# Graph layer on one core: sixteen counted groups in pairs, in slices of 20 blocks, in place of ten single ones in strips of 8

## The chip, the core and the metric

The kernel runs on one NeuronCore of a Trainium2 chip, as one launch. The time is that of the device in microseconds; of each kernel several executions are timed and their median is given. The engines are named as in the profile: PE multiplies matrices (PEld is its weight load), DVE and ACT work on vectors, POOL issues the gathers, SP issues plain transfers.

## The reference

One layer of a graph network over 12500 nodes of 256 features and 200000 edges, whose targets `dst` are sorted:

```python
h = jnp.maximum(_layernorm(x, axis=-1), 0.0)
agg = jax.ops.segment_sum(h[src], dst, num_segments=N)
z = (1.0 + eps_gin) * h + agg
t = jnp.dot(z, W1) + b1                       # 256 -> 512
t = jax.nn.relu(_batchnorm(t, g1, bt1))
conv_out = jnp.dot(t, W2) + b2                # 512 -> 256
out = x + jax.nn.relu(_batchnorm(conv_out + h, g2, bt2))
```

Each row of `agg` is a sum of the rows of h that its edges name. Rows lie anywhere in the table, so the kernel has to fetch or to count them.

## The kernel before

**Tiles and groups.** The edges are cut into 1563 tiles of 128, and these into 131 groups of 12 tiles (`GT`), one turn of the main loop each. Groups 0 to 29 (`LEAD`) gather rows of x and normalise them on ACT, while the same stage writes h into a table `h_two` of 98 blocks of 128 nodes, each feature as two f16 halves (512 columns). From group 30 on, POOL gathers from `h_two`: 12 indirect DMAs per group, 128 rows of 1 KB each (L615), into one of four buffers `gt`. `gather` is called four regular groups ahead, and its first DMA waits until PE has summed the group that held the buffer.

**A regular turn.** DVE makes one-hots `oh` of the targets two groups ahead (`edges`, L671). PE sums (`sums`, L705): 12 tiles times two halves, 24 matmuls of 128x256, weights `oh`, into a place `ps`. DVE copies the sums of the group two before to `zs` (`hold`, L764) and makes their target columns `at` (`spots`, L769); PE puts those of three before into columns (`put`, L780), DVE adds them to `zc` (`add`, L798). Each turn also forms one slice of z@W1 (`slice_of`, L808), whose statistics DVE takes (L819) and which ACT then copies out (L825) to the table `t_tab`. Puts and slices share two PSUM buffers `pz2`, so a put may have to wait until ACT has copied a slice.

**Counted groups.** Ten groups (`COUNTED`, every ninth from 41) gather nothing. For such a group PE multiplies one-hots of its edges' source blocks with one-hots of their targets, which gives a matrix of counts, and the counts with all 98 blocks of `h_two`, read in order. The work is cut into 13 strips of 8 blocks. For a strip: `mark` makes the one-hots on DVE (128x3072, L908; for the first strip of a group also L898 and L902) and has SP load 8 blocks, 1 MB, into one of three buffers (L914); `count` runs 12 matmuls of 128x256 (L927; 64 columns in the last strip) into two PSUM buffers, ACT casts both (L939); `weigh` runs 16 matmuls of 128x256 of the strip before (L958) into one PSUM total. After the last strip ACT copies the total out (L964).

**Order.** The program's order is written out by hand, one iteration per group. `RATE` of 1.6 strips per regular turn from group 31 (`BEGIN`) fixes which strips a turn has; `sums` puts the works of a turn (the puts, the slice, then count and weigh of each strip) between the tiles of its own sums on PE. A counted group's iteration has no sums. Marks of the next turn stand on DVE behind everything else of the turn. Sums are written to four places in turn, the halves of two PSUM buffers.

The lines that set the strips and the turn's works:

```python
at = {(k + 1) * n // (len(among) + 1): work for k, work in enumerate(among)}
...
spots(i - 2)
hold(i - 2)
...
upto = min(int(turns_of * RATE), len(strips))
done = sum(len(v) for v in plan.values())
plan[i] = strips[done:upto]
```

Of the kernel before, what the change touches and what calls it, by code (L numbers as in the profile page):

```python
# [18 lines left out]
P = 128  # L19
R = 4  # L20
EPS = 1e-5
GT = 12
# [8 lines left out]
COUNTED = tuple(range(41, 131, 9))  # L31
WINDOWS = 4
BLOCKS = 8
BEGIN = 31
RATE = 1.6
# [10 lines left out]
def kernel(  # L46
# [47 lines left out]
    NS = -(-NB // BLOCKS)  # L94
    c_first, c_every = COUNTED[0], COUNTED[1] - COUNTED[0]

    def counted_of(v):

        return v[:, c_first : COUNTED[-1] + 1 : c_every]

    def tiles_of(v):

        return counted_of(v[:, : NG * GT].rearrange("p (g t) -> p g t", t=GT))
# [35 lines left out]
    inner = consts.tile([P, NC, GT], F32, name="inner")  # L139
# [35 lines left out]
    vrows = consts.tile([VN, P], F32, name="vrows")  # L175
# [9 lines left out]
    with ExitStack() as es:  # L185
# [20 lines left out]
        at = 0  # L206
        for v, n in vec_list:
            nc.scalar.dma_start(vrows[at : at + n, :], v.rearrange("(k p) -> k p", p=P))
            at += n
# [49 lines left out]
        for i in range(EARLY):  # L259
# [11 lines left out]
        pw = ps_v.tile([P, NC, WINDOWS], F32, name="pw")  # L271
        nc.tensor.matmul(
            pw, lhsT=first, rhs=tiles_of(dstT).rearrange("p g (w t) -> p g w t", t=WT)[:, :, :, 0],
            start=True, stop=True,
        )
        nc.vector.tensor_tensor(
            inner.rearrange("p g (w t) -> p g w t", t=WT),
            tiles_of(dstT).rearrange("p g (w t) -> p g w t", t=WT),
            pw.unsqueeze(3).to_broadcast([P, NC, WINDOWS, WT]),
            op=OP.subtract,  # L280
        )
# [6 lines left out]
        for k, end in enumerate((P, 2 * MARGIN + 1, WD)):  # L288
# [5 lines left out]
            (inner.rearrange("p g t -> p (g t)"), 0, P, NC * GT, 2),  # L294
# [22 lines left out]

        for w in range(WINDOWS):
            side = slice(w * WD, (w + 1) * WD)
            nc.vector.scalar_tensor_tensor(  # L320
                counted_of(shift)[side], pw[side, :, w], float(-w * WD), counted_of(place)[side],
                op0=OP.add, op1=OP.subtract,
            )
# [66 lines left out]
    def fast():  # L390
# [24 lines left out]
        with ExitStack() as fs:  # L415
# [15 lines left out]
            with ExitStack() as es:  # L431
# [34 lines left out]
                near_pe = ps_i.tile([P, WIDE + NG], F32, name="col")  # L466
                col, start = near_pe[:, :WIDE], near_pe[:, WIDE:]
                nc.vector.tensor_copy(start, base)
                nc.vector.tensor_copy(col, col_i)
# [4 lines left out]
                nc.vector.tensor_scalar(shift, shift, row, None, op0=OP.add)  # L474

# [185 lines left out]
                def edges(i):  # L661
# [4 lines left out]
                    ohs[i] = sel.tile([P, GT, P], F32, name="oh", bufs=FRONT + 2)  # L666
# [995 lines left out]
```

## Time and profile before

| | before |
|---|---|
| median of 3 runs | 2405.69 us (2400.7 to 2409.59) |
| profiled execution | 2420.87 us |
| its span | 2418.9 us |
| mean granted clock of PE | 0.807 |
| first to last gather from `h_two` | 521.3 to 2194.3 us |

The profiled execution is 0.6% longer than the median. The page gives times over its span, from first to last instruction. Its part in 40 slices shows three stages: the gathers of x with the normalising (to about slice 9), the regular turns (to about slice 36), and the second product with the output. Slices are 60.5 us long; a digit is the busy share in tenths:

```profile
PE   2445565656575776677566677766767667657997
POOL 7667666675656666566656566665556656662550
PEclk9667787778687787778777887887879778779999
```

No engine stands at nine tenths in the regular turns, which makes up the most of the span. A row of groups has the line, the engine, the operation and its tiles, then after the x the count, the busy time in us, the mean ns of one, and the idle time of the engine just before with what ended it. "remote" is a release that the profile can't put down to an engine.

### The profile page before, as it was taken

To read this page: it belongs to the slowest core of one execution; us is meant where nothing else is said; L and a number is where in the kernel's file an instruction comes from. 1 tells how busy PE (TensorE), PEld (TensorE's weight loads), DVE (VectorE), ACT (ScalarE), POOL (GpSimd) and SP (SyncE) were. 2 spreads that over 40 slices of the span, in tenths; PEclk is the share of its full clock that TensorE was granted. 3 is DMA by queue.
4 is the path that set the end of the run, shared out by engine and by line. 5 is a ranking of instruction groups with operands and counts; after the bars stand their busy time and mean duration, and the time that the engine had idled before them with its cause. 6 is when DMAs were issued, how large, how long until landed. Compare 5 with 4: busy or idle time off the path is not lost.

```text
span 2418.9 us, 22189 instructions
## 1 busy us (share of the span) xinstructions
PE 1584.0 (65%) x8138; PEld 1077.9 (45%) x8138; DVE 1248.2 (52%) x1442; ACT 627.1 (26%) x1145; POOL 1451.5 (60%) x1489
## 2 busy tenths in 40 slices
PE   2445565656575776677566677766767667657997
PEld 1334454434354454445444454544434445434445
DVE  5455556545344545455354463544536455224997
ACT  4446665623111111111111111111111111102555
POOL 7667666675656666566656566665556656662550
PEclk9667787778687787778777887887879778779999
DMA  6466666554465655556456555655655556643988
GB/s 177 146 192 190 192 195 193 178 153 144 145 205 171 202 191 193 184 184 200 158 192 205 185 190 191 209 189 167 205 172 193 178 169 208 202 111 124 325 307 340
DMA packets 159092, 462.69 MB, mean 191 GB/s; under 512 B 30867, under 2 KB 58683, under 8 KB 143613
## 3 DMA queue, kind: packets, MB, share of 16 engines
q1 hardware_dynamic: 74777, 245.78, 29.3%
q0 software_dynamic: 69248, 189.16, 26.8%
q10 hardware_dynamic: 14948, 26.23, 2.9%
q8 instruction: 66, 1.08, 0.2%
q14 instruction: 53, 0.43, 0.1%
HBM read 397.00 MB, written 64.05 MB: 191 GB/s over the span
## 4 chain that ended last, share of the span: by engine, by line
PE 35%; another core or an unknown queue 27%; DVE 15%; issue 11%; ACT 10%; DMA 1%; ACTq 0%; SPq 0%; DVEq 0%
PE ps L705 8%; DVE more L908 7%; PE ph L958 6%; PE pz L808 5%; PE ph L927 4%; PE pz L780 4%; DVE oh L671 3%; ACT more L513 2%; ACT gt L513 2%; PE one L1201 2%; PE ph L808 2%; ACT gta L513 2%; PE pr L1201 1%; PE pq L1201 1%
## 5 line engine op out<-in xcount | busy, mean ns | idle before, releaser
L615 POOL DMA_INDIRECT gt<-h_two,srcT x1083 | 1025.7, 947 | 648.6 <-issue 304.5
L705 PE MATMUL ps<-gt,oh 128*128 128x256 f16 (+1 forms) x2424 | 450.6, 316 | 127.7 <-issue 114.6
L908 DVE TENSOR_TENSOR more<-col,more 128x3072 bf16<-128x3072 f32 (+1 forms) x130 | 410.3, 3166 | 231.1 <-remote 143.3
L939 ACT CAST more<-ph 128x512 f16<-128x512 f32 (+1 forms) x260 | 143.1, 562 | 1126.9 <-remote 414.5
L705 PEld LDWEIGHTS <-oh 128*128 128x128 f16 x2136 | 228.2, 108 | 234.0 <-issue 188.3
L780 PE MATMUL pz<-at,zs 128*128 128x256 f32 x476 | 169.7, 487 | 216.6 <-ACT ts L825 189.4
L764 DVE COPY zs<-ps 128x256 f32<-128x256 f32 x89 | 37.2, 418 | 498.4 <-remote 398.8
L958 PEld LDWEIGHTS <-more 128*128 128x128 f16 x1960 | 203.9, 105 | 160.3 <-issue 125.9
L958 PE MATMUL ph<-gta,more 128*128 128x256 f16 x1308 | 195.2, 297 | 73.6 <-issue 70.1
L808 PE MATMUL pz<-zc,w1s 128*128 128x512 f32 (+1 forms) x296 | 186.2, 761 | 74.9 <-DVE zc L798 52.7
L927 PE MATMUL ph<-more,more 128*128 128x256 bf16 (+1 forms) x1560 | 200.7, 277 | 33.6 <-issue 29.9
L671 DVE TENSOR_TENSOR oh<-col,dstT 128x1536 f16<-128x1536 f32 (+1 forms) x119 | 208.0, 1749 | 24.1 <-remote 17.4
L780 PEld LDWEIGHTS pz<-at,zs 128*128 128x128 f32 x476 | 107.1, 244 | 254.2 <-ACT ts L825 202.9
L615 POOL DMA_INDIRECT gt<-in_x_dram,srcT x144 | 139.9, 971 | 69.4 <-issue 39.4
L927 PEld LDWEIGHTS <-more 128*128 128x128 bf16 x1560 | 151.9, 102 | 62.9 <-issue 39.9
L808 PEld LDWEIGHTS pz<-zc,w1s 128*128 128x128 f32 x296 | 69.4, 258 | 136.0 <-issue 108.7
L958 PE MATMUL ph<-more,more 128*128 128x256 f16 x652 | 93.5, 297 | 23.1 <-issue 19.4
L798 DVE TENSOR_TENSOR zc<-pz,zc 128x512 f32<-128x512 f32 (+7 forms) x185 | 90.6, 515 | 28.6 <-remote 10.4
L808 PE MATMUL ph<-zc,w1s 128*128 128x512 f32 (+1 forms) x104 | 65.0, 753 | 56.5 <-issue 31.8
L825 ACT COPY ts<-pz 128x512 f32<-128x512 f32 x72 | 42.6, 592 | 219.1 <-DVE st L819 192.3
L615 POOL DMA_INDIRECT gta<-in_x_dram,srcT x80 | 76.5, 956 | 30.0 <-issue 16.6
L819 DVE BATCH_NORM_STATS2 st<-pz 128x6 f32<-128x512 f32 x72 | 49.8, 691 | 80.2 <-PE pz L808 31.6
(231 smaller groups left out, 1904.1 us busy)
## 6 DMA issues: line engine op xcount, KB each, us to landing
gta<-h_two SPq DMA_DIRECT2D x80, 1024.0 KB
more<-h_two SPq DMA_DIRECT2D x40, 1024.0 KB
t_tab<-ts ACTq DMA_DIRECT2D x96, 256.0 KB
gt<-h_two,srcT POOLq DMA_INDIRECT x1083
h_two<-more SPq DMA_DIRECT2D x24, 512.0 KB
h_cols<-gt SPq DMA_DIRECT2D x24, 512.0 KB
zc<-h_cols SPq DMA_DIRECT2D x24, 512.0 KB
yT<-h_cols SPq DMA_DIRECT2D x24, 512.0 KB
```

The lines of the kernel that those rows point to most:

```text
L513: nc.scalar.activation(slot(to, c), slot(v, c), AF.Relu, bias=nb[:, c : c + 1], scale=rs[:, c : c + 1])
L615: fetch = nc.gpsimd.indirect_dma_start(out=slot(ga, t - t0)[:rows], out_offset=None, in_=x if i < LEAD else h_two, in_offset=bass.Indirect ...
L671: nc.vector.tensor_tensor(oh, col[:, :P].unsqueeze(1).to_broadcast([P, n, P]), dstT[:, t0 : t0 + n].unsqueeze(2).to_broadcast([P, n, P]), ...
L705: part = nc.tensor.matmul(ps, lhsT=lhsT, rhs=side, start=(j == order[0] and side is sides[0]), stop=(j == order[-1] and side is sides[-1]),)
L780: nc.tensor.matmul(pz[:, d, :n], lhsT=zs[:, d * P : (d + 1) * P], rhs=at[:, :n], start=True, stop=True)
L798: nc.vector.tensor_add(side, pz[:, :, a - lo : b - lo], side)
L808: nc.tensor.matmul(ph[:, :n], lhsT=w1s[:, d, f * P : (f + 1) * P], rhs=zc[c][:, d, :n], start=(d == 0), stop=(d == DC - 1),)
L908: nc.vector.tensor_tensor(marks[(k * NS + s) % 3][:, :, :n], col[:, :n].unsqueeze(1).to_broadcast([P, GT, n]), keys[k % 2][:, s, :].unsque ...
L927: nc.tensor.matmul(ph[:, w * strip : w * strip + n], lhsT=low[:, j, :], rhs=marked[:, j, :n], start=(t == 0), stop=(t == WT - 1),)
L939: nc.scalar.copy(to[:, :b, 2 * v * WD : 2 * (v + 1) * WD].rearrange("p a (w d) -> p w a d", w=2), ph.rearrange("p (w a d) -> p w a d", w=2 ...
L958: nc.tensor.matmul(total, lhsT=counts[m % 2][:, a, :], rhs=nodes_of[m % 3][:, a, side * D : (side + 1) * D], start=(s == 0 and a == 0 and ...
L1201: nc.tensor.matmul(ps, lhsT=w[:, k, :], rhs=t[:, k, :], start=(k == 0), stop=(k == DC - 1))
```

## The change

Sixteen groups are counted, in eight pairs of neighbours: 43 and 44, 54 and 55, and so on every 11 to 120 and 121. Both groups of a pair are weighed by the same pass over `h_two`.

- The pass has 5 slices of 20 blocks (`BLOCKS`; 18 in the last). A node's counts have 6 windows of 21 target columns (`WINDOWS`, before 4 of 32).
- `count`: for each slice and pair 12 counts, each 2 matmuls of 128x420 (378 in the last slice) and one ACT cast. There are 960 matmuls in 480 counts, before 1560 with 260 casts.
- `weigh`: for each piece of 4 blocks (`PIECE`) 8 matmuls of 128x512, both halves at once, the two groups alternately into two PSUM totals. There are 1568, before 1960 of 128x256.
- `phase`: the counts of the next slice stand among the weighing of this one, three ahead of each piece. The works of a pair are spread evenly over the nine regular turns ahead of it by a price for each. Groups 122 and later have no such work.
- `load`: 512 KB pieces into three buffers; a piece is loaded right behind the weighing that freed its buffer. There are 200, before 130 loads of 1 MB (1024 KB).
- `mark`: 80 one-hots "a" of 128x1536 and 96 "b" of 128x840; b marks are kept for all five slices of a pair. A list made at build time puts them into turns, at most 3600 elements (`MARKS`) where the due turn allows, ahead of the turn's sums.
- The second total takes one of the two PSUM buffers of the sums, so the sums after `LEAD` alternate between the two halves of the other, and `hold` comes one turn earlier: of the group before. A counted group's hold is a DVE sum over the two halves of its total, in place of ACT's copy.
- One-hots of the targets lie in one fixed tile `hots`, whose spare part holds marks and pieces. At the start 17 more small DVE operations prepare the windows.

Gathers from `h_two` go from 1083 to 1011, and PE's own sums lose 6 x 24 = 144 matmuls.

```diff
-COUNTED = tuple(range(41, 131, 9))
-WINDOWS = 4
-BLOCKS = 8
+PAIR_AT, PAIR_EVERY, PAIRS_ = 43, 11, 8
+COUNTED = tuple(PAIR_AT + PAIR_EVERY * j + r for j in range(PAIRS_) for r in range(2))
+WINDOWS = 6
+BLOCKS = 20
+PIECE = 4
 BEGIN = 31
-RATE = 1.6
+MARKS = 3600
...
                 def sum_place(i):
+                    if i >= LEAD:
+                        if not banks:
+                            banks.append(ps_s.tile([P, 2, D], F32, name="ps"))
+                        return banks[0][:, rank[i] % 2, :]
...
                 def hold(i):
+                    zss[i] = sel.tile([P, D], F32, name="zs", bufs=3)
                     if i in COUNTED:
-                        zss[i] = held[COUNTED.index(i) % 2]
+                        both = totals[COUNTED.index(i) % 2]
+                        nc.vector.reduce_sum(
+                            zss[i], both.rearrange("p (s d) -> p d s", s=2), axis=mybir.AxisListType.X
+                        )
                         return
...
+                def phase(s):
+
+                    counting = [("count", s + 1, n) for n in range(NW)] if s + 1 < PHASES else []
+                    weighing = [("weigh", s, p) for p in pieces_of(s)]
+                    pace = -(-len(counting) // max(1, len(weighing) - 1))
+                    for k, one in enumerate(weighing):
+                        yield from counting[k * pace : (k + 1) * pace]
+                        yield one
+
+                def price(unit):
+                    return 0.42 if unit[0] == "count" else 0.44 * len(piece(unit[2]))
...
+                for i in sorted(plan):
+                    marking[i], room = [], MARKS
+                    for kind, n in list(to_mark):
...
+                        due = first_use[kind, n] <= i + 1
+                        if before < i and (room >= cost or due):
+                            marking[i].append((kind, n))
+                            to_mark.remove((kind, n))
+                            room -= cost
...
+                def load(k):
+
+                    if k < PAIRS_ * NPIECE:
+                        p = k % NPIECE
+                        a, n = p * PIECE, len(piece(p))
+                        nc.sync.dma_start(node_places[k % len(node_places)][:, :n, :], h_blocks[:, a : a + n, :])
...
+                def count(s, n):
...
+                    ph = ps_t.tile([P, CH], F32, name="ph")
+                    for t in range(WT):
+                        nc.tensor.matmul(
+                            ph[:, :wide], lhsT=a_mark[:, w * WT + t, :], rhs=b_mark[:, t, :wide],
                             start=(t == 0), stop=(t == WT - 1),
...
+                    nc.scalar.copy(
+                        counts[r][s % 2][:, : blocks(q), w * WD : (w + 1) * WD],
+                        ph[:, :wide].rearrange("p (a d) -> p a d", d=WD),
...
+                def weigh(s, p):
...
+                    for at, a in enumerate(piece(p)):
+                        for r in range(2):
                             nc.tensor.matmul(
+                                totals[r], lhsT=counts[r][s % 2][:, a % BLOCKS, :], rhs=rows[:, at, :],
+                                start=(a == 0), stop=(a == NB - 1),
                             )
+                    load(k + len(node_places))
...
                     if i >= 2:
                         spots(i - 2)
-                        hold(i - 2)
+                    while kept <= (i - 2 if kept < LEAD else i - 1):
+                        hold(kept)
+                        kept += 1
```

How the order moves is shown at two places. The first is PE within a regular turn late in the stretch, where weighing begins among the sums (before: L705 sums, L958 weigh, `ph` the total, `more3` the counts, `gta0` the node rows; the part in square brackets names what the row waits for):

```order
L927 LDWEIGHTS more3_318
L927 MATMUL ph_6508<-more1_316,more3_318 128x256
L705 LDWEIGHTS oh_6268
L705 MATMUL ps_6484<-gt_6041,oh_6268 128x256
L958 LDWEIGHTS more3_318
L958 MATMUL ph_5876<-gta0_79,more3_318 128x256 [waits DMAHW4_49]
```

The change, at such a place (L1023 count, L734 sums, L1040 weigh; `more0` and `more1` the counts of the pair's two groups, `oh_350` the tile `hots`, which also holds marks and node rows):

```order
L1023 LDWEIGHTS oh_350
L1023 MATMUL ph_5602<-gta0_79,oh_350 128x420 [waits Activation_49]
L734 LDWEIGHTS oh_350
L734 MATMUL ps_3054<-gt_5088,oh_350 128x256
L1040 LDWEIGHTS more0_336
L1040 MATMUL ph_5384<-oh_350,more0_336 128x512 [waits DMAHW7_49]
L1040 LDWEIGHTS more1_337
L1040 MATMUL ps_3099<-oh_350,more1_337 128x512
```

Rows that only repeat are left out: a matmul of one wide row takes the place of two, two totals alternate, and each count waits for an ACT cast two counts before it, which freed its PSUM buffer.

The second place is DVE over one turn. Before (L671 one-hots, L769 spots, L764 hold, L819 statistics, L798 add, L908 marks):

```order
L671 TENSOR_TENSOR oh_7025<-col_321,dstT_70 128x1536 [waits PE_49]
L769 TENSOR_SCALAR at_7027<-col_321,shift_71 128x256
L764 COPY zs_7029<-ps_6700 128x256
L819 BN_STATS st1_257<-pz2_6957 128x6 [waits PE_49]
L798 TENSOR_TENSOR zc_6132<-pz2_6950,zc_6132 128x2x256 [waits DVE_49]
L908 TENSOR_TENSOR more0_315<-col_321,more3_318 128x3072 [waits PE_49]
```

The change (L694 one-hots, L799 spots, L794 hold, L849 statistics, L828 add into two chunks, L1011 marks):

```order
L694 TENSOR_TENSOR oh_350<-col_342,dstT_70 128x1536
L799 TENSOR_SCALAR at_5993<-col_342,shift_71 128x256
L794 COPY zs_5995<-ps_3054 128x256 [waits PE_49]
L849 BN_STATS st1_278<-pz2_5903 128x6
L828 TENSOR_TENSOR zc_4976<-pz2_5898,zc_4976 128x2x128
L828 TENSOR_TENSOR zc_5331<-pz2_5898,zc_5331 128x2x128
L1011 TENSOR_TENSOR more3_339<-col_342,inner_74 128x840 x4
```

The hold now waits for PE's sums of the turn before, and what stands behind it on DVE (statistics, add, marks) waits with it; before, its sums were finished a turn earlier and it carries no wait here. The marks are four small operations in place of a large one.

More of the change, by code (lines that the diff above doesn't have):

```diff
@@ L206 @@
         at = 0
+        vrows = raw.tile([VN, P], F32, name="vrows")
         for v, n in vec_list:
@@ L852, in fast @@
                 counts = [
-                    bytes_of(t, c, c + 2).bitcast(F16).rearrange("p (a m) -> p a m", m=P)
-                    for t, c in ((more[3], 6), (more[0], 6))
-                ]
-                keys = [
-                    bytes_of(more[3], 10 + k, 11 + k)[:, : NS * GT].rearrange("p (s t) -> p s t", t=GT) for k in range(2)
-                ]
-                offsets = sel.tile([P, NS], F32, name="offsets", bufs=1)
-                block = sel.tile([P, NC, GT], F32, name="block", bufs=1)
@@ L861, in fast @@
-                key = sel.tile([P, NC, GT], F32, name="key", bufs=1)
-                nodes_of = [as_two(v) for v in (lands[0][0], lands[1][0], more[2][:, :LOW, :])]
-                assert strip == 2 * P and strip * 2 == CH and BLOCKS <= LOW
-                h_blocks = h_two.rearrange("(b a) d -> b a d", a=NB)
-                held = [more[2][:, LOW + k, :] for k in range(2)]
-                plan, strips, turns_of = {}, [(k, s) for k in range(NC) for s in range(NS)], 0
-                for i in range(BEGIN, NG - CLOSE):
-                    if i not in COUNTED:
-                        turns_of += 1
-                        upto = min(int(turns_of * RATE), len(strips))
-                        done = sum(len(v) for v in plan.values())
-                        plan[i] = strips[done:upto]
-                        assert len(plan[i]) <= 2
@@ L948, in fast @@
[L948 to L957 removed]
+                    [v.bitcast(F16).rearrange("p (a m) -> p a m", m=P) for v in of_r[:2]] for of_r in places_
+                ]
+                b_places = [of_r[2] for of_r in places_] + halves_of(more[3], *[BMARK] * 7)
@@ L958, in weigh @@
+                def weigh(s, p):
+                    if p == 0:
+                        totals[0] = ps_u.tile([P, CH], F32, name="ph")
+                    k = s // NQ * NPIECE + p
+                    rows = node_places[k % len(node_places)]
+                    for at, a in enumerate(piece(p)):
+                        for r in range(2):
                             nc.tensor.matmul(
-                                total, lhsT=counts[m % 2][:, a, :], rhs=nodes_of[m % 3][:, a, side * D : (side + 1) * D],
```

284 lines of the change are left out of this document (160 added, 124 removed).

## The prediction

> **What bounds the kernel now.** I read the page first, then the regular stretch alone, then single batches of gathers, because shares over the whole span mix three stages.
>
> ```profile
> span 2418.9 us, 22189 instructions
> PE 1584.0 (65%) x8138; PEld 1077.9 (45%) x8138; DVE 1248.2 (52%) x1442; ACT 627.1 (26%) x1145; POOL 1451.5 (60%) x1489
> PE 35%; another core or an unknown queue 27%; DVE 15%; issue 11%; ACT 10%; DMA 1%; ACTq 0%; SPq 0%; DVEq 0%
> ```
>
> The busy times and the chain that ended last name no engine that is always at work: PE leads with 65% and only 35% of the chain, and 27% went to something that the profile cannot name.
>
> ```profile
> 521.30:2194.30 1673.00, 1100.01 (x6418) 761.86 (x6419) 770.25 (x675) 230.60 (x414) 1024.73 (x1083) 0.79 0.56 181
> L615 POOL DMA_INDIRECT gt<-h_two,srcT x1083: 898/947/978, 521.3 to 2194.3; - x181
>   issue: 304.5, 999
>   PE ps L705: 198.6, 32
>   remote: 126.5, 45
> ```
>
> The first row is the stretch from the first gather out of h_two to the last: duration, busy time and instructions of PE, its weight loads, DVE, ACT and POOL, then granted clock, DMA share and GB/s. The next is POOL's gather line (shortest, median, longest ns), then what ended its idle time. The 1083 gathers make 1083/12 = 90.25 turns (a counted group has none), so a turn costs 1673/90.25 = **18.54 us**. PE is busy 1100.0/90.25 = 12.19 us of it and idle 6.35. POOL waits for PE's sums to free a gather buffer, so PE's loop paces the turns, not POOL.
>
> ```profile
> 1195.00:1200.00 5.00, 5.00 (x27) 3.31 (x26) 2.25 (x3) 0.00 (x0) 2.84 (x3) 0.89 0.74 262
> 1200.00:1205.00 5.00, 3.65 (x43) 3.07 (x40) 0.00 (x0) 0.53 (x2) 3.80 (x4) 1.00 0.35 105
> 1205.00:1210.00 5.00, 0.00 (x0) 0.00 (x0) 0.00 (x0) 0.00 (x0) 3.79 (x4) 0.64 0.36 105
> 1210.00:1215.00 5.00, 0.00 (x0) 0.00 (x0) 1.56 (x4) 0.50 (x1) 1.97 (x3) 0.50 0.36 88
> 1196.27 0.95 POOL L615 DMA_INDIRECT gt<-h_two,srcT  x1 [7.05 <-PE ps L705]
> 1197.52 0.95 POOL L615 DMA_INDIRECT gt<-h_two,srcT  x1 [0.30 <-issue]
> ...
> 1213.44 0.42 DVE L764 COPY zs<-ps 128x256 f32<-128x256 f32 x1 [16.18 <-remote]
> 1213.67 0.95 POOL L615 DMA_INDIRECT gt<-h_two,srcT  x1 [2.69 <-remote]
> 1214.50 0.59 ACT L825 COPY ts<-pz 128x512 f32<-128x512 f32 x1 [12.28 <-DVE st L819]
> 1215.14 2.08 PE L780 MATMUL pz<-at,zs 128*128 128x256 f32 x4 [11.49 <-ACT ts L825]
> ```
>
> Four windows of 5 us (same columns), and rows of the timeline. A batch of 12 gathers starts at 1196.27. PE, DVE and ACT first run, then all three stand still from 1205 to 1213 while only POOL issues; when the batch is out, DVE's hold runs first, then ACT's copy, then PE's put, which had waited 11.49 us for that copy. So a batch lets a certain amount of PE work through and holds the rest, and what is held hangs on the chain hold, statistics, copy, put.
>
> **The change part by part.** Prices, from the same views:
>
> ```profile
> L705 PE MATMUL ps<-gt,oh 128*128 128x256 f16 (+1 forms) x2136 | 376.8, 304 | 110.5 <-issue 97.4 <-DVE zs L764 10.3 <-ACT more L513 2.2
> L958 PE MATMUL ph<-gta,more 128*128 128x256 f16 x1308 | 195.2, 297 | 73.6 <-issue 70.1 <-ACT more L964 3.0
> L958 PE MATMUL ph<-more,more 128*128 128x256 f16 x652 | 93.5, 297 | 23.1 <-issue 19.4 <-ACT more L964 3.5
> L927 PE MATMUL ph<-more,more 128*128 128x256 bf16 (+1 forms) x1560 | 200.7, 277 | 33.6 <-issue 29.9 <-ACT more L939 3.2
> ...
> 1160.35 1.47 PE L927 MATMUL ph<-more,more 128*128 128x256 bf16 x12
> 1191.57 3.57 PE L958 MATMUL ph<-gta,more 128*128 128x256 f16 x16 [1.02 <-issue]
> 1200.08 0.51 PE L927 MATMUL ph<-more,more 128*128 128x64 bf16 x12
> 1200.87 1.91 PE L958 MATMUL ph<-more,more 128*128 128x256 f16 x16
> ```
>
> *Gathers.* Six more groups are counted: 72 gathers go, 1011 stay, 84.25 turns. At an unchanged turn that is 72/12 × 18.54 = **111.2 us**.
>
> *PE.* No row is wider than 256 in f16, so I extend the count rows: 0.51/12 = 0.0425 us at 64 columns and 1.47/12 = 0.1225 at 256 give 0.000417 us per column, so 0.229 at 512, 0.191 at 420, 0.173 at 378. Weighing goes from 1960 matmuls of 1.91/16 = 0.119 to 1568 of 0.229, a factor of 1.54: 288.7 us busy become 444. If the width cost nothing it would be 0.8 × 288.7 = 231; if everything ran at the slow row's 3.57/16 = 0.223, doubled, 1568 × 0.446 = 699. Counting goes from 1440 × 0.1225 + 120 × 0.0425 = 181.5 us to 768 × 0.191 + 192 × 0.173 = 179.9: the 200.7 stay 199. Own sums lose 144 matmuls of 376.8/2136 = 0.176: −25. In all 1100 + 155 − 2 − 25 = **1228 us, or 14.6 per turn** (12.0 and 17.6 at the two bounds). I take 14.6, from rows at full clock that differ in width alone. Matmuls in the stretch fall from 6418 by 392 + 600 + 144 to 5282, from 71.1 to 62.7 a turn.
>
> The Trainium skill, "TensorE: Matmul & The Clock Gate", section "Back-to-back issue gap", gives about 131 ns for each matmul of 512 columns in a stream of weight loads and matmuls. By it weighing would take 1568 × 0.131 = 205 us, PE would have less to do than before, and the sum would be that of the first rival; the trace's 0.0425 against 0.1225 us speaks for a price by columns, and no run here shows 512 columns in f16.
>
> ```profile
> L908 DVE TENSOR_TENSOR more<-col,more 128x3072 bf16<-128x3072 f32 x120 | 401.0, 3351 | 209.9 <-remote 127.8 <-PE ph L927 42.8 <-PE ph L958 29.7
> L908 DVE TENSOR_TENSOR more<-col,more 128x768 bf16<-128x768 f32 x10 | 9.5, 950 | 21.3 <-remote 15.6 <-PE ph L958 3.3 <-PE ph L927 2.4
> L902 DVE TENSOR_TENSOR more<-col,block 128x1536 bf16<-128x1536 f32 x10 | 17.5, 1749 | 0.0
> L764 DVE COPY zs<-ps 128x256 f32<-128x256 f32 x87 | 36.4, 418 | 497.3 <-remote 398.8 <-PE ps L705 98.5
> L819 DVE BATCH_NORM_STATS2 st<-pz 128x6 f32<-128x512 f32 x72 | 49.8, 691 | 80.2 <-PE pz L808 31.6 <-issue 26.1 <-remote 22.5
> L825 ACT COPY ts<-pz 128x512 f32<-128x512 f32 x72 | 42.6, 592 | 219.1 <-DVE st L819 192.3 <-issue 19.1 <-DVE at L769 4.2
> L939 ACT CAST more<-ph 128x512 f16<-128x512 f32 x240 | 137.9, 587 | 1031.9 <-remote 391.8 <-PE ph L927 344.6 <-issue 161.7
> L939 ACT CAST more<-ph 128x128 f16<-128x128 f32 x20 | 5.1, 267 | 95.0 <-PE ph L927 53.7 <-remote 22.7 <-issue 16.0
> ```
>
> *DVE.* Marks of 401 + 9.5 + 17.5 = 428 us become 80 of 1536 elements (1.749) and 96 of 840: 0.950 + 72 × (1.749 − 0.950)/768 = 1.025. That is 140 + 98 = 238. The 16 sums of two halves are new, between a hold (0.418) and statistics over 512 (0.691), at most 11 us. DVE falls by about 180 us, but it idled over half of the stretch, so I book nothing.
>
> *ACT.* 480 casts in place of 260: (0.587 − 0.267)/384 per column gives 0.510 at 420 and 0.475 at 378, 384 × 0.510 + 96 × 0.475 = 241 against 143. ACT would stand at 0.33 ms in 1.56. Hidden by its idle time; but the count buffers are two, so a third count of a run of three waits for the first cast. At worst 0.5 us for each run of three, 160 × 0.5 = 80 us.
>
> *Loads.* 200 pieces of 512 KB take the place of 130 loads of 1 MB, less in sum. Each is issued by SP behind the weighing three pieces earlier, 3 × 84.25/200 = 1.3 turns ahead; even at the slowest window's 88 GB/s one takes 6 us. SP's loads of node sums queue behind them, and these are wanted turns later. Nothing, unless pieces bunch.
>
> *The hold* comes a turn earlier, so DVE now waits for the sums that PE has just finished. Behind it on DVE stand the statistics, for them waits ACT's copy, and for that PE's next put, one tile into the following sums: 0.418 + 0.691 + 0.592 = 1.70 us of chain, of which PE covers two matmuls, 0.25. For 80 slices that is up to 116 us, 1.4 a turn; at best it lies within idle time that is there anyway.
>
> *Start.* 17 more small operations on DVE, nearest row below:
>
> ```profile
> L320 DVE SCALAR_TENSOR_TENSOR shift<-pw,place 32x10 f32<-32x10 f32 x4 | 0.7, 172 | 4.3 <-ACT below L299 4.3
> ```
>
> 17 × 0.172 = 2.9 us if none is covered; most can stand in the 4.3 us that DVE waits there. I take 1.
>
> **Sum.** Per turn PE gets 2.4 us more to do (14.6 against 12.2), 1.4 us of it could be lost at the put, and fewer instructions have to pass a batch (62.7 against 71.1). I let these cancel: idle time falls from 6.35 to 3.9 and the turn stays 18.54. In the batch above the three engines stood for 8 us with work at hand, so there is room for it. Profiled run: 2420.87 − 111.2 + 1 = 2310.7. The median of the runs is 2405.69, 0.9937 of the profiled run: 2310.7 × 0.9937 = **2296 us**.
>
> **Rivals.** *A, the turn shortens to POOL's own pace.* If what a batch lets through is counted in instructions, 12% fewer pass sooner. POOL's floor is 12 × 0.947 + 11 × 0.30 + 2.69 = 17.35 us. 84.25 × 17.35 = 1462, 211 less: 2420.87 − 211 + 1 = 2211, 2197 at the median. For it: POOL's 198.6 us of waiting for sums, and PE's work fits, 14.6 under 17.35. Against it: the put's longer chain. Chance 0.23.
>
> *B, slower.* PE's idle time of 6.35 us a turn isn't room but latency: the signals between engines come late while gathers run (the hold that stood 16.18 us), and a hold that now waits for the last sums puts that latency into every turn, behind 14.6 us of work. A turn is then 20.95, 84.25 × 20.95 = 1765, 92 more: 2514, 2498 at the median. It decides from a turn of 1672/84.25 = 19.85 us, that is, from an idle time of 5.2. For it: the put's waits on ACT's copy, and nothing shows that wider matmuls pass while everything stands. Against it: half of the idle time is one long stand in each batch, which more work can fill. Chance 0.22.
>
> In the Trainium skill, same page, section "A second HAM failure mode: psum-queue depth-cycling", a kernel with 512-wide matmuls that cycle through PSUM banks makes PE idle so briefly and often that its clock swings between half and full. The windows above show 0.50 to 1.00 already; by that rule weighing would move towards the 699 us bound, 17.6 us of PE a turn, which leads to B.
>
> *C, nothing.* A turn of 19.6 to 20.0, gathers saved and longer turns in balance. Chance 0.09. The forecast keeps 0.46. That the groups stay uncounted is no rival: the built program has 1011 gathers.
>
> **Range and chances.** A median of this kernel can be told from no change at about 0.5%, 12 us. The low end is A's, less 7: 2190. Upward the 80 us of the casts alone would give 2376 and the 116 us at the put 2411; the range takes in both, C, and turns up to 20.1 us, and stops at 2430, which leaves out most of B. Faster: 0.46 + 0.23 and a little of C, 0.71; same 0.08; slower 0.21.
>
> **What would show it.** One row of the waits (engine and line, what it waited for, us in all, times, longest):
>
> ```profile
> PE pz L780 <- ACT ts L825: 209.5, 33, 20.1
> ```
>
> In the profile after: 1011 gathers over about 1560 us; PE busy near 1230 us in them, weighing near 444 (205 to 231 would be the rule by matmuls, 700 the slow clock); DVE's waits at the hold longer and PE's wait at the put no longer than these 209.5 us (B: far more); POOL's wait for sums about as now (A: near nothing). The prediction is wrong if the matmul's width costs nothing, if the casts hold back the counts, or if the turn follows the chain behind the hold.

## The result, and the profile after

The changed kernel is slower: 2483.68 us in the median (2472.33 to 2486.0) beside 2406.66 us for the kernel before, a ratio of 1.031 with a 95% interval of 1.028 to 1.035. The forecast was 2296 us; rival B's time was 2498. The profiled execution took 2486.0 us, 65.1 more than that of before.

First the page of the changed kernel (span, then busy time of each engine), the chain that ended last, and the regular stretch from the first to the last gather out of `h_two`, with columns as before:

```profile
span 2484.1 us, 20219 instructions
PE 1668.0 (67%) x7004; PEld 960.0 (39%) x7004; DVE 1050.1 (42%) x1516; ACT 727.1 (29%) x1355; POOL 1386.0 (56%) x1417
PE 45%; another core or an unknown queue 21%; issue 13%; ACT 10%; DVE 10%; DMA 1%; ACTq 0%; SPq 0%; DVEq 0%
518.20:2260.50 1742.30, 1188.44 (x5308) 646.79 (x5309) 573.62 (x735) 330.10 (x624) 954.61 (x1011) 0.85 0.52 154
```

The stretch grew from 1673.0 to 1742.3 us, 69.3 more, which is the whole loss: it begins 3.1 us earlier, and what follows it fell from 224.6 to 223.6 us. There are 1011 gathers, 84.25 turns, so a turn went from 18.54 to **20.68 us**. PE is busy 14.1 us of it and idle 6.57 (before 6.35).

POOL's row keeps the books of a turn. It has the gathers' busy time and mean, then POOL's idle time ahead of them by what ended it; the first row is of the kernel before, the second of the changed one, each from its groups by line:

```profile
L615 POOL DMA_INDIRECT gt<-h_two,srcT x1083 | 1025.7, 947 | 648.6 <-issue 304.5 <-PE ps L705 198.6 <-remote 126.5
```

```profile
L640 POOL DMA_INDIRECT gt<-h_two,srcT x1011 | 955.5, 945 | 788.0 <-PE ps L734 457.7 <-issue 283.3 <-remote 46.7
```

Gathers and their issue are 1330 and 1239 us, 14.7 a turn in both. The rest, POOL's waits, went from 344.1 us (3.81 a turn) to 504.7 (5.99 a turn). That difference, 2.18, makes up the turn's 2.14 us. All questions below are about this wait.

Where it stands in the changed kernel, in a piece of its timeline at a pair (the gathers of one batch end at 1042.4) and in its waits (us in all, times, longest):

```profile
1034.56 0.68 DVE L789 TENSOR_REDUCE zs<-ph 128x256 f32<-128x512 f32 x1
1037.52 3.54 PE L838 MATMUL pz<-zc,w1s 128*128 128x512 f32 x4
1042.17 0.68 DVE L789 TENSOR_REDUCE zs<-ps 128x256 f32<-128x512 f32 x1
...
1059.71 0.42 DVE L794 COPY zs<-ps 128x256 f32<-128x256 f32 x1 [13.55 <-PE ps L734]
1059.94 0.94 POOL L640 DMA_INDIRECT gt<-h_two,srcT  x1 [17.59 <-PE ps L734]
1060.19 0.38 PE L734 MATMUL ps<-gt,oh 128*128 128x256 f16 x2 [0.52 <-DVE zs L794]
```

```profile
PE ph L1023 <- ACT more L1027: 123.7, 41, 7.1
PE ps L734 <- DVE zs L794: 118.6, 60, 19.7
PE pz L810 <- ACT ts L855: 83.7, 57, 6.5
```

Three suspects come from these lines. Two counted groups in a row free no gather buffer, and POOL waits 17.59 us. PE's sums now wait for the hold of the turn before (118.6 us, 60 times; before 10.3 us): both places of the sums lie in one PSUM bank, and that this could make PE wait was not in the prediction. And counts wait for casts (123.7 us). The fourth suspect is PE's 1.9 us of additional work per turn.

### The profile page after: what moved, and what is told of

The parts are those of the page before. It is cut to its first block, busy times and chain, and to the rows that moved or that the text cites. A ratio compares the mean times of both kernels' runs of the same rounds, so it can differ in the third digit from the quotient of the medians.

```text
span 2484.1 us, 20219 instructions
## 1 busy us (share of the span) xinstructions
PE 1668.0 (67%) x7004; PEld 960.0 (39%) x7004; DVE 1050.1 (42%) x1516; ACT 727.1 (29%) x1355; POOL 1386.0 (56%) x1417
## 4 chain that ended last, share of the span: by engine, by line
PE 45%; another core or an unknown queue 21%; issue 13%; ACT 10%; DVE 10%; DMA 1%; ACTq 0%; SPq 0%; DVEq 0%
PE ps L734 8%; PE ph L1023 7%; PE ps L1040 6%; PE ph L1040 6%; PE pz L838 5%; PE pz L810 4%; ACT gt L538 2%; PE one L1284 2%; ACT more L538 2%; DVE oh L694 2%; PE ph L838 2%; ACT more L1027 2%; DVE st L849 2%; PE pr L1284 1%
## 5 line engine op out<-in xcount | busy, mean ns | idle before, releaser
L640 POOL DMA_INDIRECT gt<-h_two,srcT x1011 | 955.5, 945 | 788.0 <-PE ps L734 457.7
L734 PE MATMUL ps<-gt,oh 128*128 128x256 f16 (+1 forms) x2280 | 470.2, 309 | 136.5 <-DVE zs L794 118.6
L1027 ACT CAST more<-ph 128x420 f16<-128x420 f32 (+1 forms) x480 | 242.8, 515 | 1027.3 <-remote 429.6
L794 DVE COPY zs<-ps 128x256 f32<-128x256 f32 x83 | 35.2, 424 | 1093.4 <-PE ps L734 881.2
L734 PEld LDWEIGHTS <-oh 128*128 128x128 f16 x1992 | 209.2, 105 | 332.5 <-issue 210.0
L810 PE MATMUL pz<-at,zs 128*128 128x256 f32 x516 | 175.7, 471 | 144.9 <-ACT ts L855 83.7
L1040 PEld LDWEIGHTS <-more 128*128 128x128 f16 x1568 | 170.4, 109 | 188.0 <-issue 70.1
L1040 PE MATMUL ph<-gtb,more 128*128 128x512 f16 x524 | 226.4, 432 | 0.0
L1040 PE MATMUL ps<-gtb,more 128*128 128x512 f16 x524 | 225.0, 429 | 0.0
L694 DVE TENSOR_TENSOR oh<-col,dstT 128x1536 f16<-128x1536 f32 (+1 forms) x113 | 197.5, 1749 | 1.8 <-DVE col L487 1.8
L1023 PEld LDWEIGHTS <-more 128*128 128x128 bf16 x768 | 76.2, 99 | 211.6 <-issue 199.4
L1023 PE MATMUL ph<-more,more 128*128 128x420 bf16 (+1 forms) x360 | 98.3, 358 | 87.4 <-issue 48.7
L1023 PE MATMUL ph<-gta,more 128*128 128x420 bf16 (+1 forms) x312 | 85.1, 357 | 73.7 <-issue 40.2
L828 DVE TENSOR_TENSOR zc<-pz,zc 128x512 f32<-128x512 f32 (+7 forms) x185 | 90.8, 516 | 57.3 <-issue 26.0
L1011 DVE TENSOR_TENSOR more<-col,keys 128x1536 bf16<-128x1536 f32 x64 | 111.3, 1750 | 0.6
L1040 PE MATMUL ph<-oh,more 128*128 128x512 f16 x260 | 111.1, 427 | 0.0
L1040 PE MATMUL ps<-oh,more 128*128 128x512 f16 x260 | 110.4, 425 | 0.0
```

The source lines that it names most:

```text
L640: fetch = nc.gpsimd.indirect_dma_start(out=slot(ga, t - t0)[:rows], out_offset=None, in_=x if i < LEAD else h_two, in_offset=bass.Indirect ...
L694: nc.vector.tensor_tensor(oh, col[:, :P].unsqueeze(1).to_broadcast([P, n, P]), dstT[:, t0 : t0 + n].unsqueeze(2).to_broadcast([P, n, P]), ...
L734: part = nc.tensor.matmul(ps, lhsT=lhsT, rhs=side, start=(j == order[0] and side is sides[0]), stop=(j == order[-1] and side is sides[-1]),)
L810: nc.tensor.matmul(pz[:, d, :n], lhsT=zs[:, d * P : (d + 1) * P], rhs=at[:, :n], start=True, stop=True)
L828: nc.vector.tensor_add(side, pz[:, :, a - lo : b - lo], side)
L1011: nc.vector.tensor_tensor(to, col[:, :wide].unsqueeze(1).to_broadcast([P, tiles, wide]), key.unsqueeze(2).to_broadcast([P, tiles, wide]), ...
```

## The experiments

**First four: the waits, with a PSUM bank freed.** The column numbers `col` move from PSUM to SBUF, and the free bank goes unused (e0), to the second total with a late hold (e1) or an early one (e3), or to the counts (e2). To make room, all four keep two buffers of `keys` in place of four.

```diff
-                near_pe = ps_i.tile([P, CH], F32, name="col")
-                col, start = near_pe[:, : BLOCKS * WD], near_pe[:, CH - NG :]
+                col, start = sel.tile([P, BLOCKS * WD], F32, name="colf", bufs=1), base
```

```diff
-                    totals[:] = [None, ps_s.tile([P, 2, D], F32, name="ps").rearrange("p s d -> p (s d)")]
+                    totals[:] = [None, ps_u.tile([P, CH], F32, name="ph1")]
...
-                    while kept <= (i - 2 if kept < LEAD else i - 1):
+                    while kept <= (i - 1 if kept in COUNTED or i - 1 in COUNTED else i - 2):
```

The second diff is e1's (with the sums' two banks as before); e3 leaves out its last two lines; e2 has `bufs=3` for the counts' PSUM pool.

> The changed kernel with the column numbers (the tile col, 128x420) read from SBUF and not from PSUM, which leaves one PSUM bank unused. A control for the three runs beside it. Every theory expects the changed kernel's time, 2484 us within 12; another time is the price of where col lies.

> The control, with the free bank given to the second total, so that the own sums have two banks (four places) again, and with the hold of a regular group at its old place, two turns behind. Lockstep theory (in the changed kernel each turn's sums write the bank that the hold of the last turn reads, so PE waits for DVE's hold each turn, 118.6 us in 60 waits, and the put waits behind it): 2300 to 2370, and the waits of the sums for the hold are under 20 us. Work theory (PE has 14.1 us of work per turn in place of 12.2, and idle time per turn is latency that stays): within 15 us of the control. Count theory (counts wait for ACT's casts, 123.7 us): within 15 us of the control.

> The control, with the free bank given to the counts: three PSUM buffers in place of two, so no count of a run of three waits for the cast of the first. Count theory: 100 to 125 us less than the control, the waits of counts for casts near nothing. Lockstep theory and work theory: within 15 us of the control.

> The control, with the free bank given to the second total so that the sums have two banks, and the hold still one turn behind. If the lockstep costs by the bank alone: as the run with the hold late, within 20 us. If it costs by the early hold (statistics, copy and put queued behind it): the control's time within 15 us. Work theory: within 15 us of the control.

Measured, as ratios to the kernel before with 95% intervals: e0 1.040 (1.037 to 1.042), e1 1.049 (1.046 to 1.051), e2 1.042 (1.040 to 1.044), e3 1.042 (1.039 to 1.044). But the kernel before took 2023.89 us on this chip, not 2407, and the control was paced by something else. From e0's groups by line, and its timeline:

```profile
L637 POOL DMA_INDIRECT gt<-h_two,srcT x1011 | 1110.2, 1098 | 308.1 <-issue 300.5 <-PE ph L1020 2.7 <-PE ps L1037 2.4
1199.13 1.75 DVE L691 TENSOR_TENSOR oh<-colf,dstT 128x1536 f16<-128x1536 f32 x1
1199.46 2.23 POOL L637 DMA_INDIRECT gt<-h_two,srcT  x1 [0.30 <-issue]
...
1214.09 1.75 DVE L1008 TENSOR_TENSOR more<-colf,keys 128x1536 bf16<-128x1536 f32 x1
1214.50 2.16 POOL L637 DMA_INDIRECT gt<-h_two,srcT  x1 [0.30 <-issue]
```

The same row of groups in e1:

```profile
L637 POOL DMA_INDIRECT gt<-h_two,srcT x1011 | 1127.0, 1115 | 308.0 <-issue 302.8 <-PE ph L1016 1.8 <-PE ps L727 1.5
```

POOL never waits here (7.6 us beside issue), and gathers beside DVE operations that read `colf` can take 2.2 us in place of 0.95: the mean rose from 945 to 1098 ns, 1011 x 0.153 = 155 us. All 210 gathers of over 1.1 us in e0 lie beside such an operation; beside other DVE operations, and in the changed kernel beside the same ones with `col` in PSUM, they take 0.95. So the control had a price of its own and hid the question. The Trainium skill, "SBUF — State Buffer", section "Who interferes with whom", says that a DVE instruction with two inputs in SBUF contends with a GpSimd instruction that reads SBUF; the trace agrees with that, with 2.23 us for a gather beside such an operation. Nothing on the changed kernel follows from these four but this: where POOL never waits, neither the bank nor a third count buffer shortens anything. The late hold's 17 us (e1 beside e0) are not a wait either: they are gathers stretched further, 1127.0 us busy in place of 1110.2.

**The changed kernel again, and with half of the weighing.** c1 and c2 are the changed kernel and the kernel before unaltered; c3 weighs the second group of a pair with its first and last block only:

```diff
-                        for r in range(2):
+                        for r in range(2 if a in (0, NB - 1) else 1):
```

> The changed kernel once more, on the chip of the runs beside it. In the first four runs the kernel before took 2024 us there in place of 2407, so the ratio of 1.031 must be looked at anew. If the ratio hangs on PE's work or on waits between engines that do not change from chip to chip: 1.02 to 1.045. If where signals come promptly POOL's gathers pace both kernels (12 x 1.25 = 15 us a turn), the changed kernel has 6 turns fewer and is faster: 0.95 to 0.98, and the 1.04 of the control was the price of col in SBUF (208 gathers stretched).

> The kernel before, for its profile on this chip. If POOL paces it here: gathers busy near 1083 x 0.95 us, waits of POOL for sums near nothing, and a stretch of 1083 x 1.25 = 1354 us. If PE paces it as in the first profile: 1673 us.

> The changed kernel without the second group's weighing but for its first and last block (768 of 1568 matmuls of 128x512 left out; that group's sums are then incomplete). Work theory: PE has 768 x 0.22 = 169 us less to do at full clock, and the time falls by 130 to 220 us. Lockstep and count theories: the waits of the sums for the hold (118.6 us) and of the counts for the casts (123.7 us) stay and take the place of the work; the time falls by less than 60 us. If POOL paces the kernel: no change within 15 us.

The kernel before took 2408.09 us here, c1 1.030 (1.023 to 1.038), so the result holds where the kernel before takes 2.4 ms; c2's stretch was 1666.5 us, near the first. c3 took 0.985 (0.980 to 0.989), 107 us below c1. Its groups, its stretch, and c1's stretch:

```profile
L640 POOL DMA_INDIRECT gt<-h_two,srcT x1011 | 958.4, 948 | 689.2 <-PE ps L734 337.5 <-issue 284.4 <-remote 67.3
517.10:2163.50 1646.40, 1058.14 (x4542) 594.58 (x4543) 573.50 (x735) 331.07 (x624) 957.46 (x1011) 0.80 0.54 163
518.50:2263.60 1745.10, 1187.52 (x5303) 646.58 (x5302) 573.82 (x735) 330.24 (x624) 957.32 (x1010) 0.84 0.51 154
```

129 us less of PE's busy time took 99 us from the stretch. Neither theory's band held it (130 to 220, or under 60), but 107 us lie nearer to the work: PE's work is paid for, and idle time does not swallow it. c3 leaves out 768 matmuls and as many weight loads, so it does not tell the time of the work from the number of instructions.

**Lockstep and counts once more, without moving `col`.** If the second group is not weighed at all, its bank is free without SBUF: d1 gives it to the sums with the late hold, d2 with the early one. d3 splits pieces in two and sets counts between the halves. d4 does all the work, but weighs in 128x256 with both totals in one bank, which also gives the sums two banks and the late hold. The diff has lines of d4, then one of d3:

```diff
-                            nc.tensor.matmul(
-                                totals[r], lhsT=counts[r][s % 2][:, a % BLOCKS, :], rhs=rows[:, at, :],
+                            for side in range(2):
+                                nc.tensor.matmul(
+                                    totals[r], lhsT=counts[r][s % 2][:, a % BLOCKS, :],
+                                    rhs=rows[:, at, side * D : (side + 1) * D],
...
-                    weighing = [("weigh", s, p) for p in pieces_of(s)]
+                    weighing = [("weigh", s, (p, side)) for p in pieces_of(s) for side in range(2) if halfpiece(p, side)]
```

> The half-weigh kernel (the second group of a pair is not weighed at all, its hold reads the first one's total), with the bank that becomes free given to the own sums, so that they have two banks and four places as in the kernel before, and with the hold of a regular group two turns behind again. Lockstep theory: the sums no longer wait for the hold (150.9 us in the half-weigh kernel), the time is 100 to 150 us below the half-weigh kernel's ratio of 0.985: 0.92 to 0.945. Work theory (idle time is a latency that stays whatever it hangs on): 0.975 to 0.99. Latency moved, not gone: the waits change their place and the ratio stays at 0.985.

> As the run before it, but with the hold one turn behind, as in the changed kernel. If the shared bank makes the lockstep: the same ratio as the run before it within 0.008. If the early hold does (it stands ahead of statistics, copy and put): the half-weigh kernel's 0.985 within 0.008. Work theory: 0.975 to 0.99.

> The changed kernel with pieces weighed in halves of 2 blocks and counts and half pieces in turn, so that no three counts follow each other; the same matmuls, casts and loads. Count theory: the waits of counts for casts (123.7 us) go, and the time falls by 80 to 125 us, ratio 0.98 to 1.0. Work and lockstep theories: 1.025 to 1.04.

> The changed kernel, all work done, with weighing in matmuls of 128x256 (3136 in place of 1568 of 128x512), the two totals in the halves of one bank, so that the own sums have two banks again and the hold is two turns behind. Lockstep theory: 118 us fall away, 30 to 60 us of PE work come (0.119 x 3136 = 373 us at full clock against 0.216 x 1568 = 339), ratio 0.99 to 1.01. Work theory: 1.03 to 1.06. If a batch of gathers lets a number of instructions through and not an amount of work: 3136 more PE instructions with their weight loads, ratio above 1.08.

Measured, with the kernel before at 2423.93 us: d1 0.996 (0.992 to 1.000), d2 0.993 (0.989 to 0.996), d3 1.023 (1.018 to 1.029), d4 1.070 (1.065 to 1.076). Two rows of c3's waits, then d1's POOL row and one of its waits:

```profile
PE ps L734 <- DVE zs L794: 150.9, 59, 20.6
PE pz L810 <- ACT ts L855: 83.2, 54, 9.1
```

```profile
L640 POOL DMA_INDIRECT gt<-h_two,srcT x1011 | 955.6, 945 | 702.7 <-PE ps L730 313.0 <-issue 285.1 <-remote 83.8
PE pz L806 <- ACT ts L851: 140.3, 33, 19.5
```

The sums' wait for the hold, 150.9 us in c3, is gone from d1's list, and nothing was won: the put waits 140.3 us for ACT's copy (83.2 in c3), the counts 190.1 us for casts (133.0), and POOL's idle time is 702.7 us beside 689.2. The lockstep theory falls, with the early hold (d2) as with the late one. d2, with two banks, still has 94.3 us of the sums' wait, so the shared bank was not all of its cause. "Latency moved, not gone" fits best, though d1's ratio lies above the 0.985, which is of another chip. In d3 the counts' wait for casts rose from 123.7 to 173.5 us in place of going, so runs of three counts aren't its cause; as the wait stayed, d3 doesn't show what its absence would be worth. The time stayed too. d4's stretch:

```profile
524.30:2366.90 1842.60, 1174.63 (x6843) 809.59 (x6843) 570.35 (x732) 324.96 (x623) 954.71 (x1010) 0.81 0.49 145
```

It has about the PE busy time of the changed kernel (1174.63 us, 13.9 a turn) and 1568 more pairs of weight load and matmul, and is 110 us slower than d3, which does as well as the changed kernel. Its 1.070 lies between the bands of work (up to 1.06) and of instructions (above 1.08), so it decides for neither; its weight loads are also busy longer, 809.59 us in place of d3's 653.29.

**The pairs, and the kernel before with less work.** f1 leaves out of the kernel before the weighing of strips 1 to 11 of 13. f2 to f4 do all the work: f2 spreads a pair's works over ten turns, the first counted one among them; f3 puts the two groups three turns apart; f4 does that and spreads over all eleven turns. f4's lines:

```diff
-COUNTED = tuple(PAIR_AT + PAIR_EVERY * j + r for j in range(PAIRS_) for r in range(2))
+COUNTED = tuple(PAIR_AT + PAIR_EVERY * j + APART * r for j in range(PAIRS_) for r in range(2))
...
-                    steps = list(range(begin, COUNTED[2 * j]))
-                    begin = COUNTED[2 * j + 1] + 1
+                    steps = list(range(begin, COUNTED[2 * j] + 1))
+                    begin = COUNTED[2 * j] + 1
```

> The kernel before, with the weighing of strips 1 to 11 of every counted group left out (1760 of 1960 matmuls of 128x256, 259 us of PE's busy time; the counted groups' sums are then incomplete). If PE's loop paces the kernel before, as the prediction had it: 180 to 260 us less, ratio 0.89 to 0.925. Floor theory (POOL's own pace, 14.7 us for a batch of 12 gathers and 2.7 us from batch to batch, 17.4 us, paces it already; waits for PE beyond that add only 114 us): 30 to 110 us less, ratio 0.955 to 0.988, and most batches start 17.3 to 17.7 us apart.

> The changed kernel with the counting and weighing of a pair spread over ten turns, the first counted turn among them, in place of nine: all work done, in the same order. Empty-turns theory (POOL waits 17.6 us at each pair, since no own sums free a buffer for two turns while PE has little to do, and the nine other turns carry 14 us of work): 20 to 60 us less than the changed kernel, ratio 1.005 to 1.022. If the pair costs by its chain of holds and puts alone: 1.025 to 1.035.

> The changed kernel with the two groups of a pair three turns apart (43 and 46, 54 and 57, ...), both totals held behind the first; all work done, over nine regular turns as before. Empty-turns theory: no two turns follow each other without own sums, POOL's waits of 17.6 us (8 times) fall to some 6, and the time falls by 50 to 100 us, ratio 0.99 to 1.01. Work theory: 1.02 to 1.035.

> As the run before it, with counting and weighing spread over all eleven turns, the counted ones too. Empty-turns theory: 20 to 40 us below that run, ratio 0.975 to 0.995, level with the kernel before or better. Work theory: 1.0 to 1.02, from the 18% less of counting and weighing in a regular turn.

Measured, with the kernel before at 2422.15 us: f1 1.003 (1.000 to 1.006), f2 1.035 (1.029 to 1.040), f3 1.030 (1.027 to 1.033), f4 1.013 (1.008 to 1.018). f1's stretch and its POOL row:

```profile
524.30:2213.10 1688.80, 879.48 (x4692) 594.05 (x4691) 776.20 (x688) 230.27 (x415) 1022.80 (x1082) 0.74 0.53 180
L615 POOL DMA_INDIRECT gt<-h_two,srcT x1083 | 1023.7, 945 | 666.3 <-issue 310.1 <-PE ps L705 269.3 <-remote 74.6
```

PE lost 1100.0 − 879.5 = 220 us of busy time, and the kernel before did not get faster at all, not even by the 30 to 110 us that the floor theory expected. How that can be is seen in three windows of f1 (two batches of gathers run from 1290.13 to 1320.0), after them three of the kernel before:

```profile
1290.13:1307.70 17.57, 11.23 (x76) 8.08 (x74) 14.90 (x13) 2.34 (x4) 13.21 (x14) 1.00 0.47 127
1307.70:1324.20 16.50, 0.00 (x0) 0.00 (x0) 0.00 (x0) 0.00 (x1) 9.44 (x10) 0.57 0.31 87
1324.20:1329.10 4.90, 4.27 (x21) 3.02 (x21) 4.83 (x2) 3.17 (x5) 0.00 (x0) 0.50 0.00 0
```

```profile
1196.27:1204.60 8.33, 7.38 (x61) 5.44 (x59) 0.98 (x2) 0.53 (x2) 6.50 (x7) 1.00 0.59 206
1204.60:1213.40 8.80, 0.00 (x0) 0.00 (x0) 0.00 (x0) 0.00 (x0) 4.86 (x6) 0.60 0.32 94
1213.40:1217.60 4.20, 2.46 (x7) 1.78 (x8) 4.07 (x7) 0.59 (x1) 3.01 (x4) 0.50 0.78 256
```

With less work PE freed the next buffer sooner, POOL went on with a second batch without a pause, and all three engines then stood 16.5 us in place of 8.8. The gain went into a longer stand here. Counted over the stretch, the time in which PE, DVE and ACT all stand for 1 us or more is 515 us in f1, 272 in the kernel before and 321 in the changed one, so over the stretch too f1's stands grew by about what PE's work lost.

f2 and f3 show that neither filling one counted turn nor parting the groups helps alone, and the empty-turns theory fails its bands; f3's POOL row has 807.7 us of idle time, more than the changed kernel's 788.0. Only f4, which puts the same work on 11 turns in place of 9, wins: 1.013 beside f3's 1.030, 38 us, and its POOL row has less idle time. f3 and f4 lie in the work theory's bands, and f2 in that of the pair's chain of holds and puts. f4's POOL row:

```profile
L640 POOL DMA_INDIRECT gt<-h_two,srcT x1011 | 958.5, 948 | 754.7 <-PE ps L734 375.8 <-issue 283.8 <-remote 92.2
```

**Fewer instructions at equal work.** The own sums take both halves of a row in one 128x512 matmul into a whole bank; the hold adds the halves. h1 is the changed kernel so, h2 the kernel before (its weighing widened too), h3 is f4 with wide sums; all work is done.

```diff
-                        sides = [rhs] if i < LEAD else [rhs[:, :D], rhs[:, D:]]
+                        sides = [rhs]
```

> The changed kernel, all work done, with the own sums in matmuls of 128x512 (both halves of a row at once into a whole bank, 12 weight loads and 12 matmuls a group in place of 24 and 24), and the hold a DVE sum over the two halves (about 0.69 us in place of 0.42). PE's work in columns stays, its instructions fall by 24 a turn, from 126 to 102. Instruction theory (a run of gathers lets some 110 PE instructions through, whatever their width, then PE, DVE and ACT stand until the run has landed): 80 to 140 us less than the changed kernel, ratio 0.975 to 1.0. Work theory (PE's busy time per turn sets it, 14.1 us): 1.02 to 1.035.

> The kernel before, all work done, with own sums and weighing in matmuls of 128x512 (142 PE instructions a turn become 97; columns stay). If the kernel before is at POOL's own pace, as the run without most of its weighing says (1.003): 0.98 to 1.005. If instructions pace it too: 0.93 to 0.97.

> The changed kernel with all that helped together: wide sums, the groups of a pair three turns apart, counting and weighing over all eleven turns (f4, 1.013, and wide sums); all work done. Instruction theory: 0.95 to 0.985, faster than both kernels, since six turns fewer then cost POOL's pace or a little more. Work theory: 1.0 to 1.02.

The kernel before took 2022.6 us on this chip: h1 0.957 (0.956 to 0.958), h2 1.000 (0.999 to 1.001), h3 0.9545 (0.953 to 0.956). h1's POOL row:

```profile
L640 POOL DMA_INDIRECT gt<-h_two,srcT x1011 | 955.8, 945 | 308.2 <-issue 300.3 <-PE ph L1027 3.4 <-PE ps L1044 1.8
```

POOL never waits; a turn is 1262.6/84.25 = 15.0 us, and the 72 gathers that are gone give 72 x 1.25 = 90 us, where 2022.6 − 1934.8 = 88 were measured. Here the counted groups do what they are for, and h1 and h3 beat the kernel before; the changed kernel itself was not run on this chip. h1 lies below every band, and h3 in that of instructions for another reason. In h1 PE, DVE and ACT stand 0.16 us a turn, and in h2, where they stand 1.7 us, PE's longest waits are for the gathers' rows (270.9 us in all), so these runs don't tell instructions from work where the engines stand with work at hand.

## Why the prediction was wrong

**The gathers** went as counted, 1083 to 1011. **PE's work** was 14.1 us a turn where 14.6 was forecast. The price by columns held for the weighing, 437.5 us busy where 444 was forecast (counting came to 261.9 where 199 was forecast, but its rows overlap those of the sums among which it stands): the wide weighing starts a matmul every 0.216 us at a granted clock of 1.00 (rows below, from the changed kernel's timeline), forecast 0.229.

```profile
1316.49 0.38 PE L1040 MATMUL ph<-oh,more 128*128 128x512 f16 x1
...
1318.00 0.38 PE L1040 MATMUL ps<-oh,more 128*128 128x512 f16 x1
```

Seven steps take 1.51 us. The 131 ns that the Trainium skill, "TensorE: Matmul & The Clock Gate", section "Back-to-back issue gap", gives for 512 columns is not what this kernel pays. Nor did weighing move towards the 699 us: the granted clock of the stretch rose from 0.79 to 0.85. The Trainium skill, same page, section "A second HAM failure mode: psum-queue depth-cycling", tells of a clock that swings between half and full under 512-wide matmuls that cycle through PSUM banks; the trace shows such swings, 81 spells at 0.50, but 83 in the kernel before as well, so the wide matmuls did not bring them.

**DVE** fell by 197 us (forecast 180), **ACT** rose by 99.5 (98), the loads stayed hidden: no row of the waits has weighing wait for one. The **put's** wait fell from 209.5 to 83.7 us; the forecast had it no longer than before. **POOL's** wait for sums was to stay at about 198.6 us and came to 457.7. The **start** can't be told from noise: the first gather came 3.1 us earlier than before here, and 1.5 us later in c1 than in c2.

**The step that failed** is the sum's: "I let these cancel: idle time falls from 6.35 to 3.9 and the turn stays 18.54." Idle time stayed, 6.57 us, and 1.9 us more of work made the turn 2.1 us longer. Behind it stands the reading that "PE's loop paces the turns, not POOL". f1 refutes it for the kernel before: with 220 us less on PE its time is the same, and POOL's wait for PE's sums is even longer (269.3 us beside 198.6). Such a wait does not show that PE is short of time. In the changed kernel, c3 shows that work is paid for: 98.7/129.4 = 0.76 us for each us. So the idle time was not the room that the sum took it for: of PE's 554 us of it in the changed kernel's stretch, all three engines stand for 321.

**Rival B** had the outcome and nearly the time (2498), with idle time per turn about unchanged. Its ground, that signals come late while gathers run, can be read in the traces. A signal is the update of a semaphore, by which one engine tells another that something is done, and the traces record when it comes. In the batch of the prediction two of PE's matmuls that signal end at 1202.78 and 1203.43; their signals are recorded at 1213.34 and 1213.41, and SP's load and DVE's hold, which waited for them, start at once (the profile's "remote"):

```profile
1202.61 1.04 PE L705 MATMUL ps<-gt,oh 128*128 128x256 f16 x8
...
1213.35 0.32 SPq L914 DMA_DIRECT2D more<-h_two  x1
1213.44 0.42 DVE L764 COPY zs<-ps 128x256 f32<-128x256 f32 x1 [16.18 <-remote]
```

In the stretch 235 of the 531 recorded signals of PE come over 1.5 us after the end of the last matmul that signals, and 189 of 701 in the changed kernel. All of these matmuls ended during a run of gathers or within 3 us of its end. Of the signals from other times, 66 and 241, none is late. In the runs on the chips where the kernel before takes 2023 us no signal of PE in the stretch is later than 15 ns. The trace models the ends of matmuls, so it doesn't tell a late signal from a matmul that ends late, and no run shows why it is late.

B's place was wrong: it put the latency on the early hold. d1 took that hold and the shared bank away, and POOL's idle time stayed (702.7 beside 689.2 us). The latency shows at whatever waits for PE's signals.

**Rival A** did not come here. h1, another kernel on another chip, does run at POOL's own pace: 15.0 us a turn, even below A's 17.35, which held the 2.69 us pause that does not occur there.

**Open** is what sets how much PE does ahead of a stand, and so why its idle time stayed nearly the same per turn. From the first gather of a run to the start of each stand of over 2.5 us, PE's matmuls and weight loads number 119 in the median in the kernel before, 108 in the changed one, 111 in d3, 113 in d4 and 117 in f1, which looks like a fixed count; but it is 92 in c3, 88 in f2 and 126 in c2. PE's busy time up to the stand varies as much, from 8.1 us (d4) to 11.2 (d3). So neither a count of instructions nor an amount of work is shown, and d4 and c3 don't part them. h1, which was to do it, ran where PE's signals are not late. Whether the unaltered changed kernel is faster there was not run either: e0 less its 155 us of stretched gathers would be 2106.7 − 155 = 1952 us, 0.96 of 2023.89, an estimate.

## What to carry to other kernels

An idle engine with work at hand is not spare time: ask what lets it run again, and take work away from the kernel before, as f1 did, before counting on room. A wait that is removed only helps if the latency behind it goes too: the 151 us that d1 took away came back in part at two other waits, 57 us each, and no time was won. And compare only on one chip: the same kernel took 2023 or 2408 us, and with that the bound changed from engines that stand to POOL's gathers.

## What the runs showed of the hardware

The kernel before took 2407 to 2424 us in four sets of runs and 2023 to 2024 in the two others. Runs of one set share a chip, and no two of the later five sets do, so whether the chip or the time of the runs makes the difference can't be told. In the sets at 2.4 ms PE, DVE and ACT stand together 2.9 to 3.0 us a turn in the kernel before (stands of 1 us or more), the long ones in the median until some 2.4 us after the last gather of a run has been issued; in h1 such stands are 0.16 us a turn, and gathers follow each other 0.30 us apart from first to last. With the stands go PE's late signals, by up to 22.4 us in the stretch of the kernel before, while those of DVE and ACT come within 0.5 us there; after the last gather they come as promptly as in the other sets. What makes them late in these sets the traces don't show. These traces also lack records: they hold 8239 to 10045 updates of semaphores by DMAs, those of the two other sets 30586 to 30613, so late signals are counted among recorded ones alone.

A gather that ran beside a DVE operation which reads `col` from SBUF took up to 2.53 us in place of 0.95 (e0).
